# Whole pairs instead of single tiles: the exps that VectorE works out beside ScalarE in a graph attention

## The chip, the cores and the metric

The kernel runs on one core of a Trainium2 chip. A core has five engines with a queue each, worked off in order: TensorE (PE, matmuls, with its weight loads PEld), ScalarE (ACT, functions such as exp), VectorE (DVE), GpSimd (POOL) and SyncE (SP, which here only issues DMAs). They wait for one another through semaphores. TensorE writes its results to PSUM, eight banks of 512 fp32 columns on 128 partitions; the other memory on the chip is SBUF. The metric is the device time of one execution in microseconds (us).

## What is computed

Four layers over a graph of 3,327 nodes with 128 features: attention in which the adjacency matrix is the bias, two hyperbolic layers, and a message layer. Nearly all of the time is in the first:

```python
q = (x @ Wq.T).reshape(d, n, h)          # d = 128 heads of h = 8 features
k = (x @ Wk.T).reshape(d, n, h)
v = (x @ Wv.T).reshape(d, n, h)
a = jnp.einsum('dnh,dmh->dnm', q, k) * scale
a = a + spatial_encoding + edge_encoding  # both are adj
a = jax.nn.softmax(a, axis=2)
out = jnp.einsum('dnm,dmh->dnh', a, v)
```

That is 128 heads of 3,327 x 3,327 scores, each through an exp.

## The kernel before

The projections of q, k and v are written to DRAM first, together with a bound of each row's scores that replaces the maximum of the softmax. Then comes the attention stage (from line 615), in which scores are kept transposed: keys on the partitions, queries along the columns.

**Tiles.** The queries are cut into 7 column blocks of 476 (the last has 472), the heads into 32 groups of 4, the keys into 26 tiles of 128, taken as 13 pairs. A *pair* `u` is one column block, one head group and one pair of key tiles; there are 7 x 32 x 13 = 2,912, and `q` = 0 to 12 is the place of a pair in its group. The two tiles of a pair lie in two of seven PSUM banks (`S`), which `banks(u)` hands out in turn; the eighth bank (`po`) collects the outputs of the group.

**The course of a pair.** `seed` (L660) copies the adjacency tile into the bank on VectorE, one instruction for each of the two tiles. `scores` (L666) adds the scores of one head on TensorE, two matmuls, one for each tile. `exps` (L678, L681) takes the exp of both tiles on ScalarE, straight out of the banks and into SBUF. For the next head `scores` adds the difference of two heads to what lies in the same bank (the keys of both heads are stacked, with the former head's queries negated), so that the adjacency is copied once for four heads. Each head's exp must therefore be through before the next head's scores may go into the bank. After the fourth head the bank is seeded for another pair. `values` (L719) multiplies the exps with v, with a column of ones for the softmax's sum, for the four heads side by side.

Where the two banks of a pair stand next to each other, one exp takes both (952 columns, L678). In every seventh pair they are the last and the first of the seven, and two exps of 476 columns are issued (L681).

**The order.** It is written out by hand: `tc.manual_schedule()` keeps each engine's instructions as they are issued. The loop of L790 goes by slots `i`, four for each pair, one exp a slot: head 0 of pair `u` in slot 4u, head 1 in 4u+3, head 2 in 4u+6, head 3 in 4u+9, so that three or four pairs are under way at once. In every odd slot the scores of the two slots ahead are issued and then half of the `values` of an older pair; in slots 4u+1 and 4u+2 the seeds of the next two pairs, on banks that head 3 of older pairs has just left; after the last `values` of a group, in a slot of the third pair of the next group, `store` (L727) copies `po` out. In slot 4u come also the planned pieces of other work (`behind`): transposes (L293) and maxima (L297) of squares of the adjacency for later column blocks.

**Exps on VectorE.** In pairs 0, 4 and 8 of each group (`by_hand`), the exp of head 0 of the pair's first-placed bank (row `r` = 1) is worked out on VectorE (`hand_exp`): scale and clamp out of PSUM (L692), rounding to a whole number (L694), its subtraction (L696), building the power of two (L698), four steps of a polynomial (L701), and a last one that multiplies by the power (L703), nine instructions of 476 columns. ScalarE does the other tile, one exp of 476 columns. The nine are not issued at once: two of them in slot 4u of such a pair, three in slot 4u of each that follows. As the exp comes late, `heads_of` changes places of tiles in `values`: the pair takes the next pair's first tile in place of its own late one.

Of the kernel before, what the change touches and what calls it, by code (L numbers as in the profile page):

```python
# [10 lines left out]
F32 = mybir.dt.float32  # L11
# [4 lines left out]
I32 = mybir.dt.int32  # L16
AF = mybir.ActivationFunctionType
ALU = mybir.AluOpType
# [4 lines left out]
P = 128  # L23
N = 3327
D = 128
H = 8
# [10 lines left out]
CW = 476  # L37
# [10 lines left out]

EXP_C = (753.2197875976562, 522.0919799804688, 180.93934631347656, 41.8090705871582, 7.287807941436768)
EXP_LAST = 0.0013276338577270508  # L50
EXP_BITS = 117 + 0.3594970703125
LOG2_E2 = 2.8853900817779268
EXP_LEAST = -110.0
# [27 lines left out]
def width_of(c):  # L81

    return min(CW, N + 1 - c * CW)
# [8 lines left out]
def gnn_kernel(ctx: ExitStack, tc: tile.TileContext, x, adj, Wq, Wk, Wv, Wo, embed, layer,  # L92
               embed_bias, layer_bias, weight, bias, W_in, W_out, out):
    nc = tc.nc
# [174 lines left out]
    class Square:  # L269
# [29 lines left out]
        def store(self, to=by_tile):  # L299
            nc.sync.dma_start(to[:, :, self.s * P:(self.s + 1) * P].rearrange("t p n -> p t n"), self.cols)  # L300
# [38 lines left out]
    with tc.tile_pool(name="a1", bufs=1) as a1, tc.tile_pool(name="a2", bufs=2) as a2, \  # L339
# [6 lines left out]
        h = a1.tile([P, NT, D], F32, name="h")  # L346
# [16 lines left out]
        for t0 in range(0, NT, 2):  # L363
            for s in "kq":
# [3 lines left out]
                for i in range(2):  # L368
                    t = t0 + i
                    sq = a4.tile([P, H, P], F32, name="sq")  # L370
                    for b in range(2):
                        ps = projected(s, t, b)
                        by_e = ps.rearrange("p (e i) -> p e i", e=4)
                        part = (slice(None), slice(4 * b, 4 * b + 4), slice(i * P, (i + 1) * P))
# [78 lines left out]
    with tc.tile_pool(name="d1", bufs=1) as d1, tc.tile_pool(name="d2", bufs=2) as d2, \  # L453
# [17 lines left out]
        with tc.If(loose > 0):  # L471
            for s in range(squares_of(0), NT):
                square(d2, s, d2)
            for t in range(NT):
# [5 lines left out]
                with tc.For_i(0, HEADS, 1) as d:  # L480
# [3 lines left out]
                    for r in range(2):  # L484
                        for b in range(4):
# [4 lines left out]
                                             start=True, stop=True)  # L490
# [9 lines left out]
            for c in range(NC):  # L500
                c0 = c * CW
                w = min(CW, N - c0)
# [3 lines left out]
                with tc.For_i(0, HEADS, 1) as d:  # L506
# [11 lines left out]
                    po = d_ps.tile([P, CW], F32, name="po_x")  # L518
                    for t in range(NT):
# [8 lines left out]
                                         start=(t == 0), stop=(t == NT - 1))  # L528
# [9 lines left out]
    with tc.tile_pool(name="e1", bufs=1) as e1, tc.tile_pool(name="e_adj", bufs=30) as e_adj, \  # L538
# [7 lines left out]
        VA = [e1.tile([P, NT, 4, H + 1], F32, name=f"VA{i}") for i in range(2)]  # L546

        seen = e1.tile([P, 3], F32, name="seen")
        S = e_ps.tile([P, 7, 512], F32, name="S")
        po = e_ps.tile([P, 512], F32, name="po")  # L550
# [64 lines left out]
        with tc.If(loose < 1), tc.manual_schedule():  # L615
# [10 lines left out]
            pairs = [(c, g, q) for c in range(NC) for g in range(NG) for q in range(NQ)]  # L626
            n = len(pairs)
            adj_of, shift_of, v_of, e_of, here = {}, {}, {}, {}, {}
            by_vector = deque()
# [3 lines left out]
            def banks(u):  # L633
                odd = (4 - 2 * u) % 7
                return (odd + 1) % 7, odd
# [7 lines left out]
            def touch(u, rows, x):  # L643
                of = {banks(u)[r] for r in rows}
                for y, other in touched:
                    if not of & other and x.ins.engine != y.ins.engine:
                        tc.declare_no_dep(x.ins, y.ins, reason="other banks")
                for i in of:
                    if i in last:
                        tc.add_manual_dep(x.ins, last[i].ins.name, after, reason="the same bank")  # L650
                    last[i] = x
                touched.append((x, of))

            def bank(u, r):
                return S[:, banks(u)[r], :width_of(pairs[u][0])]

            def seed(u, r):
                c, g, q = pairs[u]
                w = width_of(c)
                touch(u, [r], nc.vector.tensor_copy(bank(u, r), adj_of[c][2 * q + r][:, :w]))  # L660

            def scores(u, j):
                c, g, q = pairs[u]
                w, b = width_of(c), (c * NG + g) % 2
                for r in range(2):
# [4 lines left out]
                        tc.add_manual_dep(x.ins, here.pop(c * NG + g).ins.name, after, reason="the loads")  # L670
                    touch(u, [r], x)

            def exps(u, j):
                w, (even, odd) = width_of(pairs[u][0]), banks(u)
                e = e_of[u, j] = e_e.tile([P, 2, CW], F32, name=f"e{j}", bufs=(5, 4, 3, 2)[j])
                hand = j == 0 and by_hand(u)
                if even > odd and not hand:
                    touch(u, (0, 1), nc.scalar.activation(e[:, :, :w], S[:, odd:even + 1, :w], AF.Exp, scale=2.0))  # L678
                    return
                for r in range(1 if hand else 2):  # L680
                    touch(u, [r], nc.scalar.activation(e[:, 1 - r, :w], bank(u, r), AF.Exp, scale=2.0))  # L681

            def by_hand(u):

                return 0 <= u < n and pairs[u][2] in (0, 4, 8)

            def hand_exp(u):

                w = width_of(pairs[u][0])
                f, whole = (e_h.tile([P, CW], F32, name=f"h{i}")[:, :w] for i in range(2))  # L690
                power, e = whole.bitcast(I32), e_of[u, 0][:, 0, :w]
                touch(u, [1], nc.vector.tensor_scalar(f, bank(u, 1), LOG2_E2, EXP_LEAST, op0=ALU.mult, op1=ALU.max))  # L692
                yield
                nc.vector.tensor_scalar(whole, f, ROUNDER, ROUNDER, op0=ALU.add, op1=ALU.subtract)  # L694
                yield
                nc.vector.tensor_tensor(f, f, whole, op=ALU.subtract)  # L696
                yield
                nc.vector.tensor_scalar(power, whole, EXP_BITS, 2.0 ** 23, op0=ALU.add, op1=ALU.mult)  # L698
                for k in (4, 3, 2, 1):
                    yield  # L700
                    nc.vector.scalar_tensor_tensor(e, f if k == 4 else e, EXP_C[k], f, op0=ALU.add, op1=ALU.mult)  # L701
                yield
                nc.vector.scalar_tensor_tensor(e, e, EXP_C[0], power.bitcast(F32), op0=ALU.add, op1=ALU.mult)  # L703

            def heads_of(u, r):


                first = (u, r)
                if by_hand(u) and r == 1:
                    first = (u + 1, 0)  # L710
                elif by_hand(u - 1):
                    first = (u, 1) if r == 0 else (u - 1, 1)
                return [first] + [(u, r)] * 3

            def values(u, r):
                c, g, q = pairs[u]
                w, k = width_of(c), c * NG + g
                for j, (v, of) in enumerate(heads_of(u, r)):
                    nc.tensor.matmul(po[32 * j:32 * j + H + 1, :w], VA[k % 2][:, 2 * pairs[v][2] + of, j, :],  # L719
                                     e_of[v, j][:, 1 - of, :w], start=(q == 0 and r == 0),  # L720
                                     stop=(q == NQ - 1 and r == 1))

            def store(u):
# [60 lines left out]
            def in_slot(i):  # L784

                j = -i % 4
                return (i - 3 * j) // 4, j


            for i in range(-4, 4 * n + 15):  # L790
                u, j = in_slot(i)
                if 0 <= u < n:
                    exps(u, j)
                at = i % 4
                if i == -4:
                    seed(0, 0)
                if at == 0 and by_hand(i // 4):
                    by_vector.append(hand_exp(i // 4))
                if at == 0 and by_vector:
                    for k in range(2 if by_hand(i // 4) else 3):  # L800
                        if by_vector and next(by_vector[0], True):
                            by_vector.popleft()
                if at == 0 and i > 0:
                    for f, a in behind.pop(i // 4, ()):
                        f(*a)
                if at == 1 and (i + 3) // 4 < n:
                    seed((i + 3) // 4, 1)
                u = (i - 14) // 4
                if at == 2 and 0 <= u < n and pairs[u][2] == NQ - 1:
                    store(u)  # L810
                if at == 2 and (i + 6) // 4 < n:
                    seed((i + 6) // 4, 0)
                if at % 2:
                    for k in (1, 2):
                        u, j = in_slot(i + k)
                        if 0 <= u < n:
                            scores(u, j)
                    u, r = ((i - 11) // 4, 0) if at == 3 else ((i - 13) // 4, 1)
                    if 0 <= u < n:
                        values(u, r)  # L820
                if at == 0 and 0 <= i // 4 < n:
                    loads(i // 4)
# [98 lines left out]
    part = ctx.enter_context(tc.tile_pool(name="part", bufs=3))  # L921
# [11 lines left out]
    def arr(name, w=D):  # L933
        return big.tile([P, NT, w], F32, name=name)

    def matT(name):
        return big.tile([P, NP], F32, name=name)
# [118 lines left out]
    with tc.tile_pool(name="g1", bufs=1) as g1:  # L1056
        sm = Small(g1, "s")
        h, hT = arr("h"), matT("hT")
# [17 lines left out]
        f = sm.div(sm.artanh(yn, L1_MAX_TANH), yn)  # L1076
# [33 lines left out]
    with tc.tile_pool(name="h1", bufs=1) as h1:  # L1110
        sm = Small(h1, "s")
        h, hT = arr("h"), matT("hT")
# [12 lines left out]
        f = sm.mul(sm.div(sm.artanh(pn, L2_MAX_TANH), pn), pf)  # L1125
# [8 lines left out]
        u, rr = arr("y"), sm.new()  # L1134
# [20 lines left out]
    with tc.tile_pool(name="i1", bufs=1) as i1:  # L1155
        sm = Small(i1, "s")
        h = arr("h")
# [65 lines left out]
```

## Time and profile before

| | |
|---|---|
| median of 3 runs | 11,263.95 us (11,260.99 to 11,266.25) |
| span of the profiled execution | 11,258.3 us |
| instructions in it | 205,583 |
| attention stage, first exp to last | 454 to 10,296 us |
| DMA | 1,280.87 MB, mean 114 GB/s |

The profile is of one execution. Its page gives the busy time of each engine, the chain of work that ended last (followed back from the last instruction to what released each step), and groups of instructions: line, engine, operation, written tile <- read tiles, partitions x columns, count, busy time, mean duration, and the idle time ahead of it with what ended that. In the page's rows of 40 slices, each 281 us, ScalarE shows 9 (90% or more busy) from the third slice to the thirty-sixth, and the granted clock of TensorE 9 from the third to the thirty-seventh:

```profile
ACT  3599999999999999999999999999999999996210
...
PEclk7799999999999999999999999999999999999889
```

The costliest groups of the stage:

```profile
L678 ACT ACTIVATE e<-S 128x952 f32<-128x952 f32 (+1 forms) x9408 | 8770.7, 1185 | 27.1 <-PE S L666 25.9
L719 PE MATMUL po<-e,VA 128*9 128x476 f32 (+1 forms) x46592 | 5739.4, 565 | 19.8 <-DVE OS L727 1.1
L660 DVE COPY S<-a 128x476 f32<-128x476 f32 (+1 forms) x5824 | 3816.2, 655 | 1960.3 <-ACT e L678 1486.5
L666 PE MATMUL S<-QS,KT 64*128 64x476 f32 (+1 forms) x23296 | 4846.9, 450 | 60.4 <-DVE S L660 50.6
...
L681 ACT ACTIVATE e<-S 128x476 f32<-128x476 f32 (+1 forms) x3808 | 2438.5, 795 | 7.7 <-PE S L666 7.2
L701 DVE SCALAR_TENSOR_TENSOR e<-e,h 128x476 f32<-128x476 f32 (+1 forms) x2016 | 1400.6, 695 | 46.1
```

Durations of neighbours on ScalarE overlap: an exp is begun before the one ahead of it has ended, so the durations of a group add up to more than the engine's busy time. A matmul of `values` is recorded in two passes for each of four heads.

### The profile page before, as it was taken

The page shows a single profiled execution, that of the slowest core. Times are in us where ns is not written, and L with a number is a line of the kernel's source. Part 1 is how long each engine was busy: PE and PEld are TensorE (multiplying, and loading weights), DVE is VectorE, ACT ScalarE, POOL GpSimd, SP SyncE. Part 2 cuts the span into 40 slices and gives each one's busy share as a digit, 9 for nine tenths or more (in the row PEclk, how much of TensorE's full clock was granted, in tenths as well). Part 3 has the DMA queues.
Part 4 walks back from the last instruction along what each step waited for, and adds up shares of the span by engine and source line. Part 5 has one row for each costly group of instructions (what it writes and reads, how often), then busy time and mean ns, then how long its engine had stood idle before and what let it go on. Part 6 is the DMA issues. An engine that isn't in the chain of part 4 may idle for free.

```text
span 11258.3 us, 205583 instructions
## 1 busy us (share of the span) xinstructions
PE 10755.5 (96%) x72980; PEld 3651.8 (32%) x72980; DVE 8348.1 (74%) x13563; ACT 10112.0 (90%) x13718; POOL 2069.4 (18%) x3417
## 2 busy tenths in 40 slices
PE   4599999999999999999999999999999999998779
PEld 2133333333333333333333333333333333334444
DVE  5577877778777787777877778777777777777633
ACT  3599999999999999999999999999999999996210
POOL 5221211212112121111211222111221111111000
PEclk7799999999999999999999999999999999999889
DMA  8755555555555554555555555555554545444457
GB/s 247 247 101 97 96 97 115 100 98 96 97 116 99 100 97 82 111 97 101 99 92 116 96 102 99 92 116 96 102 92 84 108 80 85 81 84 121 158 183 272
DMA packets 732444, 1280.87 MB, mean 114 GB/s; under 512 B 190463, under 2 KB 607751, under 8 KB 714909
## 3 DMA queue, kind: packets, MB, share of 16 engines
q1 hardware_dynamic: 689528, 1138.10, 51.0%
q0 software_dynamic: 41888, 129.51, 3.9%
q8 instruction: 591, 9.68, 0.4%
q14 instruction: 437, 3.57, 0.1%
HBM read 1082.90 MB, written 184.09 MB: 113 GB/s over the span
## 4 chain that ended last, share of the span: by engine, by line
ACT 71%; issue 11%; PE 9%; DVE 3%; DMA 1%; POOL 0%; SPq 0%; DVEq 0%; POOLq 0%; ACTq 0%
ACT e L678 60%; ACT e L681 12%; PE pu L1016 5%; PE po L719 2%; PE S L666 1%; DVE e L701 1%; DVE S L660 1%; PE pu L968 0%; DMA ot<-oT_d 0%; DVE xs L1003 0%; PE pu L991 0%; DVE h L696 0%; PE pu L979 0%; DMA rows<-in_adj_dram 0%; DVE h L698 0%
## 5 line engine op out<-in xcount | busy, mean ns | idle before, releaser
L678 ACT ACTIVATE e<-S 128x952 f32<-128x952 f32 (+1 forms) x9408 | 8770.7, 1185 | 27.1 <-PE S L666 25.9
L719 PE MATMUL po<-e,VA 128*9 128x476 f32 (+1 forms) x46592 | 5739.4, 565 | 19.8 <-DVE OS L727 1.1
L660 DVE COPY S<-a 128x476 f32<-128x476 f32 (+1 forms) x5824 | 3816.2, 655 | 1960.3 <-ACT e L678 1486.5
L666 PE MATMUL S<-QS,KT 64*128 64x476 f32 (+1 forms) x23296 | 4846.9, 450 | 60.4 <-DVE S L660 50.6
L666 PEld LDWEIGHTS S<-QS,KT 64*128 64x128 f32 x23296 | 2426.4, 183 | 5175.9 <-issue 1638.6
L681 ACT ACTIVATE e<-S 128x476 f32<-128x476 f32 (+1 forms) x3808 | 2438.5, 795 | 7.7 <-PE S L666 7.2
L701 DVE SCALAR_TENSOR_TENSOR e<-e,h 128x476 f32<-128x476 f32 (+1 forms) x2016 | 1400.6, 695 | 46.1
L731 POOL DMA_DIRECT2D oT_d<-OS x896 | 471.7, 532 | 4589.4 <-DVE OS L727 4505.6
L719 PEld LDWEIGHTS po<-e,VA 128*9 128x9 f32 x46592 | 691.1, 88 | 1574.7 <-issue 1482.0
L576 POOL TENSOR_SCALAR QS<-QS 32x476 fp32r<-32x476 f32 (+1 forms) x1344 | 847.9, 631 | 1492.9 <-DMA QS<-qS_d 792.6
L692 DVE TENSOR_SCALAR h<-S 128x476 f32<-128x476 f32 (+1 forms) x672 | 439.2, 654 | 81.3 <-PE S L666 9.0
L701 DVE SCALAR_TENSOR_TENSOR e<-h 128x476 f32<-128x476 f32 (+1 forms) x672 | 452.6, 673 | 0.0
L696 DVE TENSOR_TENSOR h<-h,h 128x476 f32<-128x476 f32 (+1 forms) x672 | 443.7, 660 | 0.0
L703 DVE SCALAR_TENSOR_TENSOR e<-e,h 128x476 f32<-128x476 f32 (+1 forms) x672 | 437.3, 651 | 0.0
L134 ACT COPY uT<-pu 128x494 f32<-128x494 f32 (+1 forms) x12 | 6.5, 546 | 425.9 <-PE pu L1016 425.9
L586 POOL COPY VA<-VR 128x832 f32<-128x832 f32 x224 | 202.0, 902 | 984.8 <-DMA VR<-v_d 681.6
L1016 PE MATMUL pu<-strip,h 128*128 128x494 f32 (+2 forms) x728 | 294.0, 565 | 38.9 <-ACT h L949 38.9
L694 DVE TENSOR_SCALAR h<-h 128x476 f32<-128x476 f32 (+1 forms) x672 | 312.6, 465 | 23.2
L1016 PE MATMUL pu<-strip,y 128*128 128x494 f32 (+2 forms) x728 | 294.1, 566 | 28.9 <-DVE y L1003 17.8
L698 DVE TENSOR_SCALAR h<-h 128x476 int32<-128x476 f32 (+1 forms) x672 | 288.9, 430 | 23.0
L307 POOL TENSOR_TENSOR cols<-cols,on_all 128x256 f32<-128x256 f32 x286 | 258.4, 937 | 0.2
L293 DVE STREAM_TRANSPOSE cols<-rows 128x416 f32<-128x416 f32 x208 | 204.2, 986 | 21.4 <-DMA rows<-in_adj_dram 13.7
(186 smaller groups left out, 2449.3 us busy)
## 6 DMA issues: line engine op xcount, KB each, us to landing
KT<-kS_d SPq DMA_DIRECT2D x1792, 208.0 KB
KT<-kS_d SPq DMA_DIRECT2D x1792, 104.0 KB
VR<-v_d SPq DMA_DIRECT2D x224, 416.0 KB
strip<-adjT POOLq DMA_DIRECT2D x39, 1663.5 KB, 7.0
strip<-adjT SPq DMA_DIRECT2D x36, 1663.5 KB
QS<-qS_d SPq DMA_DIRECT2D x3072, 14.9 KB
QS<-qS_d SPq DMA_DIRECT2D x1536, 29.8 KB
adjT<-cols SPq DMA_DIRECT2D x26, 1664.0 KB
```

Source lines behind the costliest of these rows:

```text
L576: nc.gpsimd.tensor_scalar(QS[b][r0:r0 + 32, j + 1, :w], QS[b][r0:r0 + 32, j, :w].bitcast(F32), -1.0, 0.0, op0=ALU.mult, op1=ALU.add)
L660: touch(u, [r], nc.vector.tensor_copy(bank(u, r), adj_of[c][2 * q + r][:, :w]))
L666: x = nc.tensor.matmul(bank(u, r), KT[b][64 * r:64 * r + 64, max(0, j - 1), q * P:(q + 1) * P], QS[b][64 * r:64 * r + 64, j, :w], start=Fa ...
L678: touch(u, (0, 1), nc.scalar.activation(e[:, :, :w], S[:, odd:even + 1, :w], AF.Exp, scale=2.0))
L681: touch(u, [r], nc.scalar.activation(e[:, 1 - r, :w], bank(u, r), AF.Exp, scale=2.0))
L692: touch(u, [1], nc.vector.tensor_scalar(f, bank(u, 1), LOG2_E2, EXP_LEAST, op0=ALU.mult, op1=ALU.max))
L696: nc.vector.tensor_tensor(f, f, whole, op=ALU.subtract)
L701: nc.vector.scalar_tensor_tensor(e, f if k == 4 else e, EXP_C[k], f, op0=ALU.add, op1=ALU.mult)
L703: nc.vector.scalar_tensor_tensor(e, e, EXP_C[0], power.bitcast(F32), op0=ALU.add, op1=ALU.mult)
L719: nc.tensor.matmul(po[32 * j:32 * j + H + 1, :w], VA[k % 2][:, 2 * pairs[v][2] + of, j, :], e_of[v, j][:, 1 - of, :w], start=(q == 0 and r ...
L731: nc.gpsimd.dma_start(oT_d[:, d * N + c * CW:d * N + c * CW + w], o[32 * j:32 * j + H + 1, :w])
L1016: nc.tensor.matmul(pu[c][:, :w], y[:m, t, :], s[:m, c * AW:c * AW + w], start=(t == 0), stop=(t == NT - 1))
```

## The change

In pairs 0 and 6 of each group head 0 is worked out on VectorE for both tiles; ScalarE has no exp of these pairs in slot 4u. The nine steps keep their operations and take 952 columns each; only the first reads PSUM, and is issued in two pieces where the two banks don't stand side by side. The exps go to a tile of their own (`eh`, 2 buffers); `e0` has 4 buffers in place of 5, and the two tiles of intermediate results are twice as wide. In place of `heads_of`, `FIRST_HEAD` says whose head 0 a pair's `values` take: pairs 0 to 4 take the next pair's, 5 takes that of pair 0; 6 to 10 take the next pair's, 11 takes that of pair 6, and 12 its own.

The steps are issued by a budget. Steps at 952 columns count 2, the two that run faster (rounding and building the power) count 1. In slot 4u the first step of a new exp is issued first and counts 1; then steps follow, of the older exp first, until 2 are reached. So pair 0 issues the first step and the rounding; 1 the subtraction; 2 the power and the first of the polynomial; 3, 4 and 5 one step each; 6 the first step of the new exp and then the last of the old one; 7 rounding and subtraction; 8 the power and the first of the polynomial; 9 to 12 one step each, in 12 the last.

```diff
+HANDS = (0, 6)
+FIRST_HEAD = (1, 2, 3, 4, 5, 0, 7, 8, 9, 10, 11, 6, 12)
...
+            def both(u):
+
+                odd, even = banks(u)[1], banks(u)[0]
+                w = width_of(pairs[u][0])
+                if even > odd:
+                    return [((0, 1), slice(0, 2), S[:, odd:even + 1, :w])]
+                return [((r,), slice(1 - r, 2 - r), S[:, banks(u)[r]:banks(u)[r] + 1, :w]) for r in range(2)]
...
             def exps(u, j):
...
-                e = e_of[u, j] = e_e.tile([P, 2, CW], F32, name=f"e{j}", bufs=(5, 4, 3, 2)[j])
-                hand = j == 0 and by_hand(u)
...
-                for r in range(1 if hand else 2):
-                    touch(u, [r], nc.scalar.activation(e[:, 1 - r, :w], bank(u, r), AF.Exp, scale=2.0))
...
-                return 0 <= u < n and pairs[u][2] in (0, 4, 8)
+                w, hand = width_of(pairs[u][0]), by_hand(u, j)
+                e = e_of[u, j] = e_e.tile([P, 2, CW], F32, name="eh" if hand else f"e{j}",
+                                          bufs=2 if hand else (4, 4, 3, 2)[j])
+                for rows, part, x in both(u) if not hand else ():
+                    touch(u, rows, nc.scalar.activation(e[:, part, :w], x, AF.Exp, scale=2.0))
 
             def hand_exp(u):
...
-                f, whole = (e_h.tile([P, CW], F32, name=f"h{i}")[:, :w] for i in range(2))
-                power, e = whole.bitcast(I32), e_of[u, 0][:, 0, :w]
-                touch(u, [1], nc.vector.tensor_scalar(f, bank(u, 1), LOG2_E2, EXP_LEAST, op0=ALU.mult, op1=ALU.max))
-                yield
+                f, whole = (e_h.tile([P, 2, CW], F32, name=f"h{i}")[:, :, :w] for i in range(2))
+                power, e = whole.bitcast(I32), e_of[u, 0][:, :, :w]
+                for rows, part, x in both(u):
+                    touch(u, rows, nc.vector.tensor_scalar(f[:, part], x, LOG2_E2, EXP_LEAST,
+                                                           op0=ALU.mult, op1=ALU.max))
+                yield 2
...
             def values(u, r):
...
-                for j, (v, of) in enumerate(heads_of(u, r)):
+                for j in range(4):
+                    v = u - q + FIRST_HEAD[q] if j == 0 else u
...
-                if at == 0 and by_hand(i // 4):
+                done = 0
+                if at == 0 and by_hand(i // 4, 0):
                     by_vector.append(hand_exp(i // 4))
-                if at == 0 and by_vector:
-                    for k in range(2 if by_hand(i // 4) else 3):
-                        if by_vector and next(by_vector[0], True):
-                            by_vector.popleft()
+                    next(by_vector[-1])
+                    done = 1
+                while at == 0 and by_vector and done < 2:
+                    cost = next(by_vector[0], None)
+                    if cost is None:
+                        by_vector.popleft()
+                    else:
+                        done += cost
```

In the changed kernel the lines move: seeds stand at L662, scores at L668, ScalarE's exps at L692, the nine steps at L700, L703, L705, L707, L710 (four) and L712, values at L720, the store at L728, transposes at L295.

More of the change, by code (lines that the diff above doesn't have):

```diff
@@ L671, in scores @@
                     touch(u, [r], x)
-            def exps(u, j):
-                w, (even, odd) = width_of(pairs[u][0]), banks(u)
-                e = e_of[u, j] = e_e.tile([P, 2, CW], F32, name=f"e{j}", bufs=(5, 4, 3, 2)[j])
-                hand = j == 0 and by_hand(u)
-                if even > odd and not hand:
-                    touch(u, (0, 1), nc.scalar.activation(e[:, :, :w], S[:, odd:even + 1, :w], AF.Exp, scale=2.0))
-                    return
-                for r in range(1 if hand else 2):
-                    touch(u, [r], nc.scalar.activation(e[:, 1 - r, :w], bank(u, r), AF.Exp, scale=2.0))
@@ L683, in by_hand @@
-            def by_hand(u):
-                return 0 <= u < n and pairs[u][2] in (0, 4, 8)
+            def both(u):
[4 more added lines that the diff above has]
+                return [((r,), slice(1 - r, 2 - r), S[:, banks(u)[r]:banks(u)[r] + 1, :w]) for r in range(2)]
+            def by_hand(u, j):
+                return j == 0 and 0 <= u < n and pairs[u][2] in HANDS
@@ L694, in hand_exp @@
+                yield 2
                 nc.vector.tensor_scalar(whole, f, ROUNDER, ROUNDER, op0=ALU.add, op1=ALU.subtract)
-                yield
+                yield 1
                 nc.vector.tensor_tensor(f, f, whole, op=ALU.subtract)
-                yield
+                yield 2
                 nc.vector.tensor_scalar(power, whole, EXP_BITS, 2.0 ** 23, op0=ALU.add, op1=ALU.mult)
+                yield 1
                 for k in (4, 3, 2, 1):
-                    yield
                     nc.vector.scalar_tensor_tensor(e, f if k == 4 else e, EXP_C[k], f, op0=ALU.add, op1=ALU.mult)
-                yield
+                    yield 2
@@ L703, in hand_exp @@
                 nc.vector.scalar_tensor_tensor(e, e, EXP_C[0], power.bitcast(F32), op0=ALU.add, op1=ALU.mult)
[L705 to L713, printed above, removed]
+                yield 2
             def values(u, r):
@@ L717, in values @@
                 w, k = width_of(c), c * NG + g
-                for j, (v, of) in enumerate(heads_of(u, r)):
-                    nc.tensor.matmul(po[32 * j:32 * j + H + 1, :w], VA[k % 2][:, 2 * pairs[v][2] + of, j, :],
-                                     e_of[v, j][:, 1 - of, :w], start=(q == 0 and r == 0),
+                for j in range(4):
+                    v = u - q + FIRST_HEAD[q] if j == 0 else u
+                    nc.tensor.matmul(po[32 * j:32 * j + H + 1, :w], VA[k % 2][:, 2 * pairs[v][2] + r, j, :],
+                                     e_of[v, j][:, 1 - r, :w], start=(q == 0 and r == 0),
                                      stop=(q == NQ - 1 and r == 1))
```

## The prediction

> **What bounds the kernel now.** I read the page first, for the engines and the chain that ended last; then the stretch of the attention stage alone (first exp at 454 us, last at 10,296 us); then who ScalarE waited for in it; then one VectorE exp in the order of time.
>
> ```profile
> PE 10755.5 (96%) x72980; PEld 3651.8 (32%) x72980; DVE 8348.1 (74%) x13563; ACT 10112.0 (90%) x13718; POOL 2069.4 (18%) x3417
> ...
> ACT e L678 60%; ACT e L681 12%; PE pu L1016 5%; PE po L719 2%; PE S L666 1%; DVE e L701 1%; DVE S L660 1%; PE pu L968 0%; DMA ot<-oT_d 0%; DVE xs L1003 0%; PE pu L991 0%; DVE h L696 0%; PE pu L979 0%; DMA rows<-in_adj_dram 0%; DVE h L698 0%
> ```
> ```profile
> 454.00:10297.00 9843.00, 9784.12 (x69874) 3116.72 (x69878) 7695.35 (x12400) 9807.39 (x13216) 1863.56 (x3100) 1.00 0.54 97
> ```
> ```profile
> ACT e L678 <- PE S L666: 16.6, 32, 1.4
> ACT e L681 <- PE S L666: 4.8, 1, 4.8
> ```
> PE looks busier than ScalarE over the whole span, but matmuls overlap. The chain is ScalarE's exps: 72% of the span. In the stage (second fence: length, then PE, PEld, DVE, ACT, POOL busy) ScalarE is busy 9,807 of 9,843 us, and all its waits there come to some 21 us. So the stage lasts as long as its exps, at full clock (1.00).
>
> What an exp costs is not its row's mean (1,185 and 795 ns), since one starts before the one ahead ends. In the trace's single entries the end of an exp follows the last end by 0.857 us if it is wide (952 elements) and 0.459 if narrow (476), in the median. Check: 9,408 x 0.857 + 3,808 x 0.459 = 9,811 us, the stage. An exp that had to wait takes 0.96 from start to end (the row's shortest is 953 ns).
>
> **What the change takes from ScalarE.** 672 narrow exps go to VectorE before; afterwards 448 whole pairs do. Of the 11,648 exps of pairs 11,200 are left, a seventh of them in two pieces: 9,600 wide and 3,200 narrow, 9,600 x 0.857 + 3,200 x 0.459 = 9,696 us, 115 less. The Trainium skill (ScalarE: Activation LUTs, What ACT_TABLE_LOAD costs) prices an exp at 186 ns + 0.833 a column, 93 overlapping: 886 and 490 ns, which makes the stage 10,200 us before, 357 over what was measured, and the gain 127. The row decides: 115.
>
> **The round that a missing turn shortens.** ScalarE takes four turns a pair; head 0 of pair u is turn 4u, head 1 turn 4u+3, head 2 4u+6, head 3 4u+9. TensorE goes in rounds of two turns: scores of turns 4u and 4u+1, values, scores of 4u+2 and 4u+3, values. One VectorE exp before:
>
> ```profile
> start us, us, engine line op out<-in xcount [idle before <-releaser]
> 5039.96 2.87 ACT L678 ACTIVATE e<-S 128x952 f32<-128x952 f32 x3
> ...
> 5041.15 1.42 DVE L660 COPY S<-a 128x476 f32<-128x476 f32 x2 [0.81 <-ACT e L678]
> ...
> 5041.74 0.82 PE L666 MATMUL S<-QS,KT 64*128 64x476 f32 x4
> ...
> 5042.48 0.99 PE L719 MATMUL po<-e,VA 128*9 128x476 f32 x8
> 5042.49 0.80 ACT L681 ACTIVATE e<-S 128x476 f32<-128x476 f32 x1
> 5042.67 0.65 DVE L692 TENSOR_SCALAR h<-S 128x476 f32<-128x476 f32 x1
> 5042.93 2.93 ACT L678 ACTIVATE e<-S 128x952 f32<-128x952 f32 x3
> 5043.36 0.52 DVE L694 TENSOR_SCALAR h<-h 128x476 f32<-128x476 f32 x1
> 5043.40 0.30 PEld L666 LDWEIGHTS S<-QS,KT 64*128 64x128 f32 x4 [0.80 <-ACT e L681]
> 5043.40 0.69 PE L666 MATMUL S<-QS,KT 64*128 64x476 f32 x4
> ...
> 5044.18 1.42 DVE L660 COPY S<-a 128x476 f32<-128x476 f32 x2 [0.30 <-ACT e L678]
> ```
> Count from the end of turn 4u-3, 5041.11. Its bank is seeded at 0.03, takes 0.66, and 0.05 later the second score of turn 4u starts: 0.74. The next of the same half follows at 1.06 (0.32), values at 1.36 (0.30; the line says 1.37), scores of turn 4u+2 at 2.26 (0.90). A score reaches a waiting exp 0.52 after its start, and the exp takes 0.96: turn 4u+2 ends at **3.74** at the earliest. ScalarE has five turns to end by then: with all wide 5 x 0.857 = 4.29, with the narrow one of today 4 x 0.857 + 0.459 = 3.89. Both are longer than 3.74, so today's missing half turn costs nothing. Afterwards the whole turn 4u is missing: 3.43. ScalarE stands 0.31 us. Where turns beside it fall on pairs in two pieces (0.92 instead of 0.857) this is 0.16 to 0.26; over the seven positions 0.27. 448 x 0.27 = **121 us**.
>
> **VectorE's queue.** Rows at 476 columns: 0.654 (L692), 0.467 (L694), 0.664, 0.434, 0.678, 3 x 0.697, 0.652. No wide one is in the trace; the nearest slope is from L703 (476 columns, 0.652) to the reduce of L297 (832, 1.009), 1.0 ns a column, so 476 more cost 0.48. L694 and L698 pass about two columns in that time (their rows are 0.2 shorter): 0.24. Ends: 0.40 (a wide one hides some of it) and 0.52. A pair is then 9.5 us, 19 a group in place of 17; over the stage 450 us more, 83% busy. Its total does not bind. Two rules of the skill pull apart here: VectorE: DVE Perf Modes (The TRN2 errata) asks for tiles of 512 columns and more, for the fixed cost is paid once an instruction; Perfetto Trace Analysis (Optimizing Scalar/DVE Operations) says that where VectorE isn't saturated, but causes bubbles on other engines, breaking up instructions may bring work forward. By the first alone the sum is -115. VectorE is 78% busy, so the second applies; its price, from the queue:
>
> The two seeds start at 0.03 and 0.79, the first step at 1.55 (today 5042.67, the same). It is wide: the next may start at 2.72. Head 1 of this pair waits for it, but only for turn 4u+3, whose scores start at 2.75 in place of 2.58: 2.75 + 0.52 + 0.96 = 4.23, before 3.74 + 0.857. Free. Behind it stands:
> - Pair 0: the rounding step, dependent, 0.57 to the next start: 3.31. The seed due at the end of turn 4u+1 (2.57) starts there: 3.31 + 0.66 + 0.05 + 0.52 + 0.96 = 5.50 for turn 4u+4, against 3.74 + 2 x 0.857 = 5.45. 224 x 0.04 = **9 us**.
> - Pair 6: the last step of pair 0's exp, 1.04: the seed starts at 3.76 and turn 4u+4 ends at 5.95: 0.50, with two-piece positions 0.40. 224 x 0.40 = **90 us**.
> - Pair 7: rounding and subtraction end at 6.85 when the next seed is due at 6.84. But in 88 groups (176 transposes of L293 in the stage, half of them at this pair) a transpose, 0.91, comes between: 0.91 late, of which 0.34 is slack (2.57 - 0.03 - 0.66 - 0.05 - 0.52 - 0.96): 88 x 0.57 = **50 us**.
>
> Elsewhere a pair issues at most 1.7 us beside its seeds' 1.4, under a pair's 3.43 on ScalarE; with the store of L727 (pair 2) or a reduce (pair 12) that is 3.5 to 3.8, over by less than the slack and the pair after can take. Values of pair 5 read pair 0's exps, whose last step ends 3.8 us after the end of turn 4u-3 of pair 6; they stand nine turns further. Head 0's four buffers: last read in the values issued at turn 4u+13, written again at 4u+16. If that cover went, each would cost up to a turn, 0.86. Matmuls, DMAs and GpSimd's work keep number and place.
>
> Sum: -115 + 121 + 9 + 90 + 50 = +155, and some 5 for first steps in two pieces (64 of 448): **+160**. The same walk with 0.40 in place of 0.48 gives pair 6 0.24 and the transposes 0.45, +105; with 0.52, 0.48, 0.60 and 0.06 at pair 0, +185. Span 11,258.3 + 160 = 11,418; runs take 5.65 more (11,263.95): **11,424 us**, 1.4% slower. ScalarE's exps, fewer, no longer set the pace in two pairs of thirteen.
>
> **Rivals.**
> 1. Faster: every wait fits into slack, 11,264 - 115 = 11,149. For it: today's starts run 0.2 ahead of need (1,185 against 960 ns). Against: the 3.74 has no other path. It decides if that path is really shorter than 3.43, four turns, and VectorE's seeds come back within the 0.34 of slack. 5%.
> 2. Level: VectorE's wide steps cost only half as much again, so that seeds are hardly held and the round's 121 stand against 115: 11,270. For it: VectorE waits 1,568 us of the stage for ScalarE today before its seeds. Against: that idle time lies in other pairs than 0 and 6, and no row is cheaper than 1.0 ns a column but rounding and power. 6%.
> 3. VectorE falls further behind: GpSimd's steps beside it already stretch L694 from 0.41 to 0.52; at 0.56 more per wide step pair 0 costs 0.10, pair 6 0.58 and a transpose 0.66: -115 + 121 + 22 + 130 + 58 + 5 = +221, and with the second seed of pair 7 late too some 11,500. 16%.
>
> The forecast, 11,370 to 11,480 for itself, has 68%, and 5% lie between it and the rivals. The range 11,335 to 11,505 leaves out rivals 1 and 2 and the upper part of 3. Under 0.2% (22 us) can't be told from no change: faster 0.05, same 0.05, slower 0.90.
>
> **What would show it.** ScalarE 12,800 exps, and waits for scores of some 270 us in place of 21; VectorE's wide steps at 1.13 to 1.18 (rounding and power 0.7); seeds of L662 that start up to 1.2 us after their bank is free, behind L712. Wrong, if ScalarE has no such waits, or if they stand elsewhere than one and four turns behind the missing one.

## The result

| | before | changed |
|---|---|---|
| median of 4 runs each | 11,263.42 us | 11,416.93 us (11,414.11 to 11,421.26) |
| ratio | | 1.0138, 95% interval 1.0125 to 1.015 |
| span of the profiled execution | 11,258.3 us | 11,412.6 us |
| attention stage, end of the first exp to end of the last | 454.3 to 10,296.1 us | 461.4 to 10,450.3 us |

The kernel is 1.4% slower. Of the 154 us between the profiled executions 147 are in the attention stage, which went from 9,842 to 9,989 us; it also began 7 us later. The page of the changed kernel, with the lines that answer to those shown before (engine totals, the chain that ended last by line, groups):

```profile
PE 10896.4 (95%) x72980; PEld 3680.5 (32%) x72980; DVE 8794.5 (77%) x11611; ACT 10094.6 (88%) x13302; POOL 2305.3 (20%) x3417
...
PE po L720 35%; PE S L668 30%; ACT e L692 6%; PE pu L1022 5%; DMA QS<-qS_d 4%; DMA KT<-kS_d 4%; DVE S L662 2%; DVE cols L295 1%; DVE OS L728 1%; SPq L566 1%; DVE eh L710 0%; DVE h L700 0%; PE pu L974 0%; DVE h L703 0%; PE ps_y L918 0%
...
L692 ACT ACTIVATE e<-S 128x952 f32<-128x952 f32 (+3 forms) x12800 | 9790.2, 976 | 199.7 <-PE S L668 183.2
...
L662 DVE COPY S<-a 128x476 f32<-128x476 f32 (+1 forms) x5824 | 3812.1, 655 | 1767.9 <-ACT e L692 1433.5
```

ScalarE has its 12,800 exps, and idles 183 us before them for scores where it idled 26 and 7. The row's mean of 976 ns takes wide and narrow exps together; the wide ones alone fell from 1,185 to 1,072 ns, the narrow ones from 795 to 687. That is no faster exp: one that starts after a wait has no other ahead of it that is still running, and a wide one then takes 0.96 us (the median of 712 of them). The groups of the wide steps, each shape apart (the window is the stage):

```profile
L710 DVE SCALAR_TENSOR_TENSOR eh<-eh,h 128x952 f32<-128x952 f32 x1152 | 1381.0, 1199 | 0.0
...
L710 DVE SCALAR_TENSOR_TENSOR eh<-h 128x952 f32<-128x952 f32 x384 | 465.2, 1211 | 0.0
L705 DVE TENSOR_TENSOR h<-h,h 128x952 f32<-128x952 f32 x384 | 448.0, 1167 | 6.6
L712 DVE SCALAR_TENSOR_TENSOR eh<-eh,h 128x952 f32<-128x952 f32 x384 | 447.9, 1166 | 0.0
L700 DVE TENSOR_SCALAR h<-S 128x952 f32<-128x952 f32 x328 | 377.1, 1150 | 36.3 <-PE S L668 1.5
L707 DVE TENSOR_SCALAR h<-h 128x952 int32<-128x952 f32 x384 | 259.6, 676 | 0.0
L703 DVE TENSOR_SCALAR h<-h 128x952 f32<-128x952 f32 x384 | 253.8, 661 | 6.6
```

A step at 952 columns takes 1.15 to 1.21 us, 0.50 to 0.53 more than at 476; rounding (L703) and the power (L707) take 0.66 and 0.68.

**Where ScalarE stands.** Idle time ahead of exps is too short a measure, because exps are begun ahead and a delay first eats that lead. The ends tell it all. A *late end* is an exp's end less the end of the one before, less 0.857 us for a wide and 0.459 for a narrow one. Here they are summed over the stage by turn within the group of 13 pairs (worked out from the trace's single entries, here and in all later tables):

| late ends of exps, us in the stage | before | changed |
|---|---|---|
| second exp behind pair 0's missing turn (turn 4u+2) | 1 | 75 |
| fourth exp behind it (4u+4) | 1 | 26 |
| second exp behind pair 6's | 0 | 70 |
| fourth exp behind it | 2 | 68 |
| eighth and twelfth behind it | 0 | 54 |
| pairs 10 and 11 | 18 | 0 |
| all but those of the stage's first five pairs (10 and 3) | 22 | 290 |

With the first five pairs they grew from 32 to 294 us, by 262; less the 115 that ScalarE no longer works, that is the stage's 147. This sum has to come out, for a late end is what the stage has beyond its exps' own times; what it tells is the place. Past the start of the stage, the waits stand two, four, eight and twelve turns behind the missing ones and nowhere else. One pair 6 of the changed kernel, in the order of time (start, length, engine and line, idle time before; lines left out are marked):

```profile
5394.29 1.42 DVE L662 COPY S<-a 128x476 f32<-128x476 f32 x2 [0.63 <-ACT e L692]
...
5394.78 0.93 PE L668 MATMUL S<-QS,KT 64*128 64x476 f32 x4
...
5395.64 0.98 PE L720 MATMUL po<-e,VA 128*9 128x476 f32 x8
5395.81 1.15 DVE L700 TENSOR_SCALAR h<-S 128x952 f32<-128x952 f32 x1
...
5396.56 0.94 PE L668 MATMUL S<-QS,KT 64*128 64x476 f32 x4
...
5396.88 1.14 DVE L712 SCALAR_TENSOR_TENSOR eh<-eh,h 128x952 f32<-128x952 f32 x1
5397.02 0.18 PEld L668 LDWEIGHTS S<-QS,KT 64*128 64x128 f32 x2 [0.28 <-DVE h L700]
...
5397.43 0.99 PE L720 MATMUL po<-e,VA 128*9 128x476 f32 x8
...
5397.94 1.41 DVE L662 COPY S<-a 128x476 f32<-128x476 f32 x2
...
5398.35 0.99 PE L668 MATMUL S<-QS,KT 64*128 64x476 f32 x4
...
5399.16 3.54 ACT L692 ACTIVATE e<-S 128x952 f32<-128x952 f32 x4 [0.26 <-PE S L668]
```

Turn 4u-3 ended at 5394.26; times below count from this end. Seeds, scores, values and scores of the round follow as they did before the change (5394.29, 5394.78, 5395.64, 5396.56). The first step (L700) ends at 5396.96, and the weight load of the scores of turn 4u+3 (5397.02) has waited for it. The old exp's last step (L712) follows, and behind it the seeds start at 5397.94, 3.68 us after the origin, although the bank of the first had been left at 2.24 (at 2.57 in most groups, where that exp takes both tiles at once). The exp that needed this seed starts late, at 5399.16.

### The profile page after: what moved, and what is told of

The parts are those of the page before. It is cut to its first block, busy times and chain, and to the rows that moved or that the text cites. A ratio compares the mean times of both kernels' runs of the same rounds, so it can differ in the third digit from the quotient of the medians.

```text
span 11412.6 us, 204701 instructions
## 1 busy us (share of the span) xinstructions
PE 10896.4 (95%) x72980; PEld 3680.5 (32%) x72980; DVE 8794.5 (77%) x11611; ACT 10094.6 (88%) x13302; POOL 2305.3 (20%) x3417
## 4 chain that ended last, share of the span: by engine, by line
PE 71%; DMA 9%; ACT 7%; DVE 6%; issue 3%; SPq 1%; POOL 0%; DVEq 0%; POOLq 0%; ACTq 0%
PE po L720 35%; PE S L668 30%; ACT e L692 6%; PE pu L1022 5%; DMA QS<-qS_d 4%; DMA KT<-kS_d 4%; DVE S L662 2%; DVE cols L295 1%; DVE OS L728 1%; SPq L566 1%; DVE eh L710 0%; DVE h L700 0%; PE pu L974 0%; DVE h L703 0%; PE ps_y L918 0%
## 5 line engine op out<-in xcount | busy, mean ns | idle before, releaser
L692 ACT ACTIVATE e<-S 128x952 f32<-128x952 f32 (+3 forms) x12800 | 9790.2, 976 | 199.7 <-PE S L668 183.2
L720 PE MATMUL po<-e,VA 128*9 128x476 f32 (+1 forms) x44800 | 5730.9, 564 | 20.0 <-DVE OS L728 2.1
L662 DVE COPY S<-a 128x476 f32<-128x476 f32 (+1 forms) x5824 | 3812.1, 655 | 1767.9 <-ACT e L692 1433.5
L668 PE MATMUL S<-QS,KT 64*128 64x476 f32 (+1 forms) x23296 | 4986.7, 452 | 72.1 <-DVE S L662 63.5
L668 PEld LDWEIGHTS S<-QS,KT 64*128 64x128 f32 x23296 | 2452.8, 183 | 5294.5 <-ACT e L692 2547.9
L710 DVE SCALAR_TENSOR_TENSOR eh<-eh,h 128x952 f32<-128x952 f32 (+1 forms) x1344 | 1605.1, 1194 | 0.0
L578 POOL TENSOR_SCALAR QS<-QS 32x476 fp32r<-32x476 f32 (+1 forms) x1344 | 994.8, 740 | 1498.7 <-DMA QS<-qS_d 846.2
L720 PEld LDWEIGHTS po<-e,VA 128*9 128x9 f32 x44800 | 684.9, 88 | 1303.7 <-issue 1211.1
L720 PE MATMUL po<-eh,VA 128*9 128x476 f32 (+1 forms) x1792 | 865.0, 564 | 0.0
L700 DVE TENSOR_SCALAR h<-S 128x952 f32<-128x952 f32 (+3 forms) x512 | 518.7, 1024 | 49.4 <-PE S L668 1.5
L710 DVE SCALAR_TENSOR_TENSOR eh<-h 128x952 f32<-128x952 f32 (+1 forms) x448 | 539.2, 1203 | 0.0
L705 DVE TENSOR_TENSOR h<-h,h 128x952 f32<-128x952 f32 (+1 forms) x448 | 520.8, 1163 | 7.7
L712 DVE SCALAR_TENSOR_TENSOR eh<-eh,h 128x952 f32<-128x952 f32 (+1 forms) x448 | 521.1, 1163 | 0.0
L707 DVE TENSOR_SCALAR h<-h 128x952 int32<-128x952 f32 (+1 forms) x448 | 302.0, 674 | 0.0
L703 DVE TENSOR_SCALAR h<-h 128x952 f32<-128x952 f32 (+1 forms) x448 | 295.2, 659 | 7.7
L295 DVE STREAM_TRANSPOSE cols<-rows 128x416 f32<-128x416 f32 x208 | 204.0, 986 | 22.0 <-DMA rows<-in_adj_dram 14.1
```

The costliest lines, as they stand in the source:

```text
L295: nc.vector.transpose(self.cols[:, t0:t0 + NQ, 32 * j:32 * j + 32], self.rows.rearrange("p (x t) -> p t x", t=NT)[:, t0:t0 + NQ, :])
L578: nc.gpsimd.tensor_scalar(QS[b][r0:r0 + 32, j + 1, :w], QS[b][r0:r0 + 32, j, :w].bitcast(F32), -1.0, 0.0, op0=ALU.mult, op1=ALU.add)
L668: x = nc.tensor.matmul(bank(u, r), KT[b][64 * r:64 * r + 64, max(0, j - 1), q * P:(q + 1) * P], QS[b][64 * r:64 * r + 64, j, :w], start=Fa ...
L692: touch(u, rows, nc.scalar.activation(e[:, part, :w], x, AF.Exp, scale=2.0))
L700: touch(u, rows, nc.vector.tensor_scalar(f[:, part], x, LOG2_E2, EXP_LEAST, op0=ALU.mult, op1=ALU.max))
```

## The experiments

Three things stand together at a missing turn: TensorE's round, the wide first step, and the steps queued behind it. The first four runs take them apart.

**First step only.** Steps two to nine are taken out of `hand_exp`; the first writes the exps' tile.

```diff
...
-                    touch(u, rows, nc.vector.tensor_scalar(f[:, part], x, LOG2_E2, EXP_LEAST,
+                    touch(u, rows, nc.vector.tensor_scalar(e[:, part], x, LOG2_E2, EXP_LEAST,
                                                            op0=ALU.mult, op1=ALU.max))
-                yield 2
-                nc.vector.tensor_scalar(whole, f, ROUNDER, ROUNDER, op0=ALU.add, op1=ALU.subtract)
...
-                nc.vector.scalar_tensor_tensor(e, e, EXP_C[0], power.bitcast(F32), op0=ALU.add, op1=ALU.mult)
                 yield 2
```

> Steps two to nine of the exps on VectorE are left out (pairs 0 and 6 pass on scaled scores); the missing turn and the wide first step stay. Theory (two causes: TensorE's round is shorter of one turn, and VectorE's queue holds the seeds behind a wide step): only the round is left, ScalarE loses some 145 us at the second exp behind the missing turn, in both pairs, and no more than 10 at the fourth; span about 11,280. Rival (VectorE's queue alone makes the waits, the round has slack): no waits, 11,258 - 115, some 11,145.

**No values in between.** At pairs 0 and 6 TensorE leaves out the half of an older pair's values that stands between the scores of turns 4u+1 and 4u+2.

```diff
-                    if 0 <= u < n:
+                    if 0 <= u < n and not (at == 3 and by_hand((i + 1) // 4, 0)):
                         values(u, r)
```

> The half of the values that TensorE works between the scores of turns 4u+1 and 4u+2 is left out at pairs 0 and 6 (448 of 5,824 calls); all of VectorE's steps stay. Theory: the wait at the second exp (145 us) goes, but the path through VectorE starts at the same exp and runs beside the round, so that the wait moves to the fourth exp, some 0.4 us at pair 0 and 0.6 at pair 6: span about 11,410, within 20 of the changed kernel. Rival (the two causes are worth what they show, one after the other): 145 less, some 11,267.

**Both out** has both edits.

> Both: steps two to nine and the half of the values in between are left out. Theory: neither path is left but the wide first step itself, whose end at 2.7 us still holds the scores of turn 4u+3 and with them the round after; some 0.25 us at the fourth exp, 110 us in all: span about 11,245. If the two paths were all: 11,258 - 115, some 11,145. Rival (something else than round and queue, such as the total of VectorE's work or the banks): stays above 11,300 although the work is gone.

**Pair 0 only.**

```diff
-HANDS = (0, 6)
-FIRST_HEAD = (1, 2, 3, 4, 5, 0, 7, 8, 9, 10, 11, 6, 12)
+HANDS = (0,)
+FIRST_HEAD = (1, 2, 3, 4, 5, 0, 6, 7, 8, 9, 10, 11, 12)
```

> Only pair 0 of each group goes to VectorE; ScalarE has 11,424 exps of pairs, 9,890 us. Theory (order, not load): pair 0 loses what it lost in the changed kernel, 75 us at the second exp and 26 at the fourth: stage 9,890 + 101 + 22, span about 11,430, slower than the changed kernel with half of its VectorE work. Rival (the waits come from VectorE's load, 84% busy in the changed kernel's stage): at some 62% they vanish, span about 11,330.

Measured on one chip, one execution each (the kernel before took 11,260.16 us there), late ends as above:

| | changed | first step only | no values between | both out | pair 0 only |
|---|---|---|---|---|---|
| span, us | 11,412.6 | 11,301.5 | 11,409.4 | 11,289.1 | 11,408.6 |
| second exp behind pair 0's turn | 75 | 76 | 0 | 0 | 76 |
| fourth | 26 | 26 | 95 | 93 | 27 |
| second exp behind pair 6's turn | 70 | 70 | 0 | 0 | - |
| fourth | 68 | 19 | 138 | 80 | - |
| eighth and twelfth | 54 | 0 | 53 | 0 | - |

- The waits at the second exp are the round's: they are the same without eight of nine VectorE steps (146 us of 145), and zero without the values in between.
- They are worth nothing by themselves. Without the values the kernel takes 3 us less, not 145, for the wait moves whole to the fourth exp (26 to 95, 68 to 138): the paths through TensorE and through VectorE start at the same exp and run side by side. The span was expected at about 11,410.
- VectorE's load isn't the cause of pair 0's waits. In the stage it is busy 8,138 of 9,990 us in the changed kernel (81%, where the expectation had 84) and 6,171 of 9,989 with pair 0 only (62%), and pair 0's waits are the same. The expectation was 20 us too long, since waits elsewhere in the stage (18 us in pairs 10 and 11 before) went too. With one exp in place of two the kernel takes the same time to 4 us: the second gives back all that it takes off ScalarE.
- Two expectations were missed at one place. With the first step only, 26 and 19 us were left at the fourth exp where no more than 10 were expected; with both out, 173 where 110 were. In both runs, as in the changed kernel, pair 0's scores of turn 4u+4 start at 4.15 us in the median; pair 6's start at 4.08. With both out the second exp ends on time, at 3.43 in place of 3.8, so that the same scores make the fourth later by that. Pair 0's 26 cannot come from the rounding step behind the first, as I had it, for that step is gone.

**A narrow first step.** Is what is left at the fourth exp the first step's own length? The edit is against the run with the first step only. It halves the work of that step; the other tile's exp is left out and not moved to another instruction.

```diff
-                for rows, part, x in both(u):
-                    touch(u, rows, nc.vector.tensor_scalar(e[:, part], x, LOG2_E2, EXP_LEAST,
-                                                           op0=ALU.mult, op1=ALU.max))
+                touch(u, [1], nc.vector.tensor_scalar(e[:, 0], bank(u, 1), LOG2_E2, EXP_LEAST,
+                                                      op0=ALU.mult, op1=ALU.max))
...
-                                     e_of[v, j][:, 1 - r, :w], start=(q == 0 and r == 0),
+                                     e_of[v, j][:, 0 if by_hand(v, j) else 1 - r, :w], start=(q == 0 and r == 0),
```

> As the run with the first step only, and in pairs 0 and 6 that step reads one of the two tiles; the exp of the other is left out (its bank goes on to the next head's scores at once, and the values read the one half twice). It is open where the 45 us come from that were left at the fourth exp without steps two to nine (26 at pair 0, 19 at pair 6). Theory now: the wide first step ends at 2.70 us and holds the scores of turn 4u+3 by 0.2 to 0.3, which takes nothing from that turn's own exp, but the scores of turn 4u+4 stand behind them and the values; with a narrow step (end at 2.21) the waits at the fourth exp go, those at the second stay (145): span 11,301 - 45, some 11,257. Rival (the wait is left over from the round alone, which starts late): the 45 stay, 11,301.

The span of the one execution was 11,258.6 us (the kernel before had a median time of 11,261.14 on that chip), the late ends 76 and 70 at the second exps and 0 at both fourths. The stage's busy time with the first step wide, and narrow (length; PE, PEld, DVE, ACT and POOL busy with their instructions; clock, DMA share, GB/s), in this order:

```profile
457.00:10342.00 9885.00, 9858.35 (x69866) 3136.85 (x69870) 4703.30 (x6860) 9770.70 (x12800) 1711.09 (x3096) 1.00 0.54 97
```
```profile
458.00:10296.00 9838.00, 9815.03 (x69870) 3164.53 (x69874) 4478.89 (x6796) 9732.50 (x12799) 1710.61 (x3096) 1.00 0.54 97
```

The stage is 47 us shorter (the span 43) with the same exps on ScalarE. The traces show how, in medians. A wide first step starts at 1.55 us and ends at 2.70, and the scores of turn 4u+3 start at 2.76; behind the narrow one they start at 2.61, on the heels of those of 4u+2 (2.29). One round on, with the values in between, the scores of turn 4u+4 start at 4.15 (pair 0) and 4.08 (pair 6) behind the wide step, with or without the steps that follow it, and at 3.83 behind the narrow one.

**The last step a pair earlier.** This is the full computation; pair 6 no longer has the old exp's last step between its first step and the seeds.

```diff
-                while at == 0 and by_vector and done < 2:
+                while at == 0 and by_vector and done < (4 if i // 4 % NQ in (5, 12) else 2):
```

> The computation is the changed kernel's; in pairs 5 and 12 the budget is 4 instead of 2, so that the last step of an exp is issued a pair earlier and pair 6 no longer queues it between its first step and the seed. Theory: the wait of pair 6 at the fourth exp falls from 68 us to pair 0's 26 or less, those of pairs 7 and 8 (54 us, transposes behind a late queue) to under 20; pair 5 or 6 gets some 15 back; the round's 145 stay: some 80 to 115 less than the changed kernel, ratio to the kernel before 1.004 to 1.007. Rival (the round and VectorE's load make the waits): as the changed kernel, 1.0138 within 0.001.

The median was 11,354.17 us, ratio to before 1.0081 (1.0064 to 1.0098), 63 us less than the changed kernel, where I expected 80 to 115. What was to go went: 68 to 27 at the fourth exp behind pair 6's turn, 54 to 0 at the eighth and twelfth. But pair 5 now issues two dependent steps of 1.19, and the seeds in it start 0.17 us after their bank is free instead of 0.03. Pair 6 starts late by it: 25 us at its first exp behind the missing turn, and 87 at the second instead of 70. That gives back 41, where I had put 15.

**Two half turns for one wide exp.** If the whole missing turn and the wide step ahead of a seed are what costs, not wide steps as such, an exp over two tiles should pay when these come from two pairs.

```diff
-HANDS = (0, 6)
+SETS = ((0, 2), (6, 8))
+HANDS = {q: (s, part) for s in SETS for part, q in enumerate(s)}
+LATE = {14: (0, 1), 15: (2, 1), 24: (6, 1), 25: (8, 1)}
...
+            def first_step(u):
+
+                w, (s, part) = width_of(pairs[u][0]), HANDS[pairs[u][2]]
+                if part == 0:
+                    late_of[u // NQ, s] = e_e.tile([P, 2, CW], F32, name="eh", bufs=2)[:, :, :w]
+                touch(u, [1], nc.vector.tensor_scalar(late_of[u // NQ, s][:, part], bank(u, 1), LOG2_E2, EXP_LEAST,
+                                                      op0=ALU.mult, op1=ALU.max))
...
-                    by_vector.append(hand_exp(i // 4))
-                    next(by_vector[-1])
-                    done = 1
+                    first_step(i // 4)
+                    if HANDS[pairs[i // 4][2]][1] == 1:
+                        by_vector.append(hand_exp(i // 4))
```

`LATE` says at which of the 26 half values of a group the late tiles are taken, and a table in place of the 2 gives the budget of each pair; the other steps of `hand_exp` stay wide.

> Full computation, another arrangement: one tile each of pairs 0 and 2, and of 6 and 8, goes to VectorE; the first step is narrow and issued in each of the two pairs, the other eight are wide over both tiles; ScalarE keeps a narrow exp in each of these turns. ScalarE: 9,216 wide and 3,968 narrow exps, 9,216 x 0.857 + 3,968 x 0.459 = 9,719 us, 92 less than before. Theory (what costs is the whole missing turn and a wide step ahead of a due seed, not wide steps as such): waits as before the change, some 22 us, span 11,166, ratio to the kernel before 0.992. Rival (wide steps on VectorE hold the seeds wherever they stand, with as much VectorE work as in the changed kernel): 100 to 150 us of waits at pairs 0 to 10, 11,270 to 11,320, ratio 1.001 or more.

The median was 11,193.64 us, ratio to the kernel before 0.9941 (0.9924 to 0.9957), faster than both. Its stage:

```profile
455.00:10226.00 9771.00, 9722.24 (x69874) 3063.72 (x69878) 8252.50 (x10833) 9737.14 (x13185) 2226.66 (x3100) 1.00 0.55 98
```

ScalarE is busy 9,737 of 9,771 us with VectorE at 84%, more than in the changed kernel. The late ends are 48 us (without the first five pairs) where 22 were expected, and the span is 21 us longer than expected. 37 of the 48 stand at one place, the second exp behind pair 2's half turn. There the scores of turn 4u+1 start at 1.06 and 1.29 us, and at 0.91 and 1.07 at pairs 0, 6 and 8; what holds them wasn't followed. Wide steps as such thus don't make the waits. The run changes the turn, the first step and the budget at once, so it doesn't say what each is worth.

## Why the prediction was right, step by step

The forecast was 11,424 us and the range 11,335 to 11,505; 11,417 was measured, and all three rivals fell. The mechanism and the places of the waits were forecast; what makes pair 0's fourth exp late was not. That the sum fits to some 6 us is luck, for its terms miss by up to 24 and the misses cancel. The measured terms come to 158 us, and the spans differ by 154:

| term | forecast | measured |
|---|---|---|
| exps taken from ScalarE | -115 | -115 (12,800 exps, in the median 0.856 and 0.459 us from end to end) |
| TensorE's round, both pairs | 121 | 145 |
| fourth exp behind pair 0 | 9 | 26, of another cause |
| fourth exp behind pair 6 | 90 | 68 |
| pair 7's transposes | 50 | 52 |
| first steps in two pieces | 5 | not told apart |
| waits of before that went (pairs 10 and 11) | 0 | -18, why wasn't followed |

- **The round.** Place, path and order of size were right, and the run without the values shows the path. It cost 0.32 us a pair in place of 0.27: scores of turn 4u+2 start at 2.29 where I had 2.26 and their exp ends at 3.78 to 3.80 where I had 3.74, and pairs in two pieces take less off than I averaged (0.23 to 0.38 over the positions, where I had 0.16 to 0.31).
- **"Head 1 of this pair waits for it ... Free."** This step failed. I asked whether the exp behind those scores would be late; it isn't. But TensorE works in order, and its values and the next round stand behind the scores that wait. It costs 45 us (26 and 19), which the run with the narrow first step removes. The 9 us that I gave to pair 0's rounding step stood at the right place with the wrong cause.
- **Pair 6's last step.** It starts at 2.62, not 2.72, and the seed at 3.68, not 3.76; and even with no step in between TensorE reaches the scores of turn 4u+4 only at 4.08, so that 19 us of the lateness were there already. Behind the late seed the second of these scores starts at 4.38. What the queue adds is 68 - 19 = 49 us, not 90.
- **Transposes.** 88 groups had one of L295 at this pair in the trace. They lost 47 us at the eighth exp and 5 at the twelfth, 0.59 each; the other 136 lost 3 in all. The forecast was 88 times 0.57.
- **The width.** 476 columns more take 0.50 us in place of 0.48 (0.53 in the first step of the polynomial, just past the end of 0.52), and 0.19 to 0.24 in the two short steps. VectorE's share of the stage was 81%, not 83, since I had divided by the shorter stage of before.
- **What would show it.** "Waits for scores of some 270 us" was right as 290 us of late ends, but I named the wrong view for it: idle time before exps shows 183. The sign of being wrong, waits "elsewhere than one and four turns behind the missing one", was written more narrowly than the sum: the sum's own places are two and four turns behind for the round and the queue, and eight for pair 7's transposes, and there the waits stand.

The rule that I let decide (the Trainium skill, Perfetto Trace Analysis, Optimizing Scalar/DVE Operations: break up instructions of an engine that isn't saturated but makes others wait) fits the one step on which TensorE waits: narrow, it gave 47 us, though in that run its other half was left out and not issued as a second instruction. For the eight other steps the rule for large tiles (VectorE: DVE Perf Modes, The TRN2 errata: large tiles spread a fixed cost of each instruction) was no hindrance: they are wide in the version that beats the kernel before. Narrow ones were not tried there, so no run here says which of the two rules those eight obey.

## What to carry to other kernels

Work taken off the bounding engine shortens its turn, and every round of other engines that was hidden under that turn must still fit: compare the longest path from one of its results to a later one with the time that is left, before counting the gain. Here, a piece taken out of each of four turns of a group kept the cover that two whole turns lost. And ask of a wait not only whether the one who waits becomes late, but what is queued behind it.

## What the runs showed that I had not expected

The chain of waits can change sides although ScalarE stays all but full. In the last run, where ScalarE is busy 9,737 of 9,771 us, the chain by line reads:

```profile
PE po L733 45%; PE S L673 35%; PE pu L1034 5%; ACT e L697 3%; DVE OS L740 1%; DMA QS<-qS_d 1%; DMA KT<-kS_d 0%; DVE S L667 0%; PE pu L986 0%; DVE xs L1021 0%; POOL a L608 0%; PE ps_y L930 0%; PE pu L997 0%; PE pu L1009 0%; DVE h L714 0%
```

3% of exps, where the kernel before showed 72%. TensorE and ScalarE are both busy nearly all of this stage (9,722 and 9,737 us), and the chain can follow either; the ends of the exps, 50 us late in all, say that ScalarE is still what the stage lasts for.

GpSimd's work in the stage, the same instructions each time, grew with VectorE's: 1,711 us busy with the first step only (VectorE 4,703), 1,864 before (7,695), 2,095 in the changed kernel (8,138) and 2,227 in the last run (8,253); its negations of queries took 0.58 us in the mean with the first step only, 0.63 before, 0.74 changed and 0.83 in the last run. In the changed kernel's trace the 550 of them that overlapped none of the wide steps took 0.59 us at the most, and so did the 168 beside the first step, the rounding or the power alone; those beside the steps with two tensor operands (L705, L710, L712) took up to 1.6. Before, some beside the rounding step of a single tile took up to 0.82, and no run takes the steps apart. ScalarE's exps waited for none of it in the changed kernel.
